# Splitting a scan chunk's rows 3 to 5 between VectorE and GpSimd, with C in two fixed PSUM banks

## The chip, the cores and the metric

The kernel runs on one core of a Trainium2 chip. The metric is the device time of one execution in microseconds (us), as a median of several runs. Engine names in the profile are PE (TensorE), DVE (VectorE), ACT (ScalarE), POOL (GpSimd) and SP (the engine that issues most DMAs).

## The reference, cut to what matters

Two layers work on eight images of 128 x 128 points with 128 channels, x[8, 128, 128, 128] in float32. The first is a linear attention with a layer norm. The second is a state-space layer with 256 inner channels and one state per channel. The change lies in the second layer's scan and the sum of its directions:

```python
xf = xb.reshape(Bb, Cd, L)
xt = jnp.transpose(xb, (0, 1, 3, 2)).reshape(Bb, Cd, L)
xs = jnp.stack([xf, xf[..., ::-1], xt, xt[..., ::-1]], axis=1)
...
dA = jnp.exp(dlt[..., None] * A[:, None])
xc = dA * xc + dut[..., None] * Bt[:, :, None, :]
y = jnp.einsum('kbcn,kbn->kbc', xc, Ct)
...
y = (y0 + y1 + y2 + y3).transpose(0, 2, 1)
yz = y * jax.nn.silu(z)
yn = gamma * (yz - mean(yz)) / sqrt(var(yz) + 1e-05) + beta
out = yn @ Wout
```

Every image is scanned along its rows and along its columns, forwards and backwards. Each scan's state is multiplied by C, which is one number for each point and the same for all channels, and the four results are added after they are turned back into one order of points. The last four lines are written shorter here than in the program.

## The kernel before, in words

There are three stages, one after the other: `layer0`, `layer1_front` and `layer1_scan`. The change is in `layer1_scan`, which the profile shows from about 4530 us to the end.

The 256 channels lie as 2 x 128 partitions. The sum `y` of one image, [128, 2, 16384], stays in SBUF. The work is a list of 8 x 4 slots, one for each image and each of its scans, and each slot is cut into 16 chunks of 1024 points, eight rows of 128. One chunk is one `step`; there are 512, and some 17 more in which the last image leaves. `place` (0 to 3) is the position of a slot in its image. The slot at place 0 writes `y`, and those at places 1, 2 and 3 add to it. In places 1 and 2 the points of the scan run along the other axis than the memory of `y` does; the program calls that `y_turned`. Then neighbours in the scan lie 128 elements (512 bytes) apart in `y`. At place 3 they don't.

In step n each engine does this, in an order written out by hand in `step`, which `in_order` keeps for each engine:

- PE makes the step sizes in PSUM (`delta`, L934) and spreads C over all partitions (`spread`, L967), one matmul for each half of a chunk.
- ACT makes softplus (`soften`, L938) and the decay (`decay`, L942) in place in PSUM, with a table load for each.
- POOL multiplies the input by the step sizes into `h` (`weigh`, L951), two instructions of 1024.
- DVE runs two scans over `h` (`scan`, L959 forwards, L961 with the other direction's views).

In the next step the chunk is given out. `emit` multiplies half of `h` (four rows, 2 x 512 elements) by C, on DVE. For the half that comes first the product goes to a PSUM buffer that the decays have left (L989 where y is turned, L993 where it isn't), and `gather` (L1001, DVE) adds it to `y`. The other half is multiplied in place (L982, DVE), and `add` (L1009, POOL) adds it to `y`, with one instruction of 512 elements for each half of the channels. So DVE adds four rows and POOL four. At place 0 both halves are written to `y` by DVE directly (L979).

The scan buffer `h` has two copies. The scan of chunk n starts from the last column of chunk n-1, so the copy of n-1 is free for n+1 only when both scans of n are done.

While the next image is at place 0, the image before leaves, one chunk in each step: `gate` (L1029) multiplies by z, `square` (L1032), `moments` (L1042) sums over the channels on PE, `keep` (L1048), `to_tokens` (L1054) turns the sums, `square_mean` (L1058) and `variance` (L1062) read them, `project` (L1074) is the output matmul, `store` (L1080) scales and stores. Such a step is called a leaving step.

[...] The pool `px` has three buffers of two banks each. The pool `pe` has two tags of one bank each. `spread` takes "pc" for the half that is emitted first and "pt" for the other, and the leaving image's `pm` and `pq` also take "pt":

```python
half1 = units[n][0].first
spread(n, half1, "pc")
spread(n, 1 - half1, "pt")
...
pm = pe.tile([P, GN], F32, name="pm", tag="pt")
pts[m] = p = pe.tile([P, GW, NC2, 2], F32, name="pq", tag="pt")
```

Of the kernel before, what the change touches and what calls it, by code (L numbers as in the profile page):

```python
# [8 lines left out]
F32 = mybir.dt.float32  # L9
BF16 = mybir.dt.bfloat16  # L10
AF = mybir.ActivationFunctionType
ALU = mybir.AluOpType
# [4 lines left out]
P = 128  # L17
B = 8
H = W = 128
L = H * W  # L20
NH, HD = 4, 32
NC2 = 2
R = 8
K = 4
GW = 4
GN = GW * H
# [5 lines left out]
CW = CH // H  # L32
NCH = L // CH
# [714 lines left out]
def layer1_scan(ctx: ExitStack, tc, ubs, xps, zs, gs, dtw, dtb, a_log, gamma, beta, w_out, out):  # L748
# [15 lines left out]
    nc = tc.nc  # L764
# [4 lines left out]
    px = ctx.enter_context(tc.tile_pool(name="l2px", bufs=3, space=PSUM))  # L769
    pe = ctx.enter_context(tc.tile_pool(name="l2pe", bufs=1, space=PSUM))  # L770
# [14 lines left out]
    for dst, src, rows in ((wparts, dtw.rearrange("k r d -> r k d"), R), (bparts, dtb.rearrange("o (k d) -> o k d", d=D2), 1)):  # L785
        x = wp.tile([rows, K, D2], F32, name="w32", tag="sp", bufs=2)
        nc.sync.dma_start(x, src)
        q = wp.tile([rows, 3, K, D2], BF16, name="w16", tag="h", bufs=2)
# [13 lines left out]
    rws, dws = [], []  # L802
    for i in range(3):
        t = const.tile([P, CH], BF16, name=f"rows{i}")
# [3 lines left out]
    for i in range(3):  # L808
        t = const.tile([P, D2], BF16, name=f"dtw{i}")
        nc.gpsimd.memset(t, 0.0)  # L810
        dws.append(t)
    csel = const.tile([P, P], BF16, name="csel")
# [17 lines left out]
    for j in range(2):  # L830
        for hf in range(2):
            at = 32 * (2 * j + hf)
            nc.vector.memset(sel[at : at + 1, hf, j : j + 1], 1.0)
    pb = pe.tile([P, P], F32, name="pbw", tag="pt")
    for c in range(NC2):
        bt = wp.tile([P, P], F32, name="bt", tag="z", bufs=6)
        nc.vector.tensor_copy(bt, gb[:, 1, c : c + 1].to_broadcast([P, P]))
# [2 lines left out]
    nc.vector.tensor_copy(bw, pb)  # L840
    for c in range(NC2):
        nc.vector.tensor_scalar(wg[:, c, :], wg[:, c, :], gb[:, 0, c : c + 1], None, ALU.mult)
    pb = pe.tile([P, P], F32, name="pbm", tag="pt")
    for c in range(NC2):
        nc.tensor.matmul(pb, means, wg[:, c, :], start=(c == 0), stop=(c == NC2 - 1))
    for c in range(NC2):
# [2 lines left out]
    y = big.tile([P, NC2, L], F32, name="y")  # L849
    yturn = y.rearrange("p c (w h) -> p c h w", h=H)  # L850

    class Slot:


        def __init__(self, n, o, s):
            self.o, self.s = o, s
            self.b, self.k = o // 4 + 2 * s, o % 4
            self.back = self.k % 2 == 1
            self.order = NAT if self.k >= 2 else TURN
            self.permuted = self.order != (TURN if self.b < B // 2 else NAT)  # L860
            self.dt_image, dt_dir = 2 * self.k + self.b // 4, self.b % 4
            self.dt_order = NAT if dt_dir >= 2 else TURN
            self.dt_turned_back = self.back != (dt_dir % 2 == 1)
            self.y_turned = (self.order == TURN) != (s < 2)
            self.y_back = s % 2 == 1
            self.place = n % K

            self.first = 1 if self.place and not self.back else 0
            self.dw = dws[n % 3]

        def weights(self):
# [8 lines left out]

            return NCH - 1 - i if self.back else i

        def y_at(self, i, hf):

            m = 2 * self.at(i) + hf
            if self.y_back:
                m = 2 * NCH - 1 - m
            if self.y_turned:
                v = yturn[:, :, m * GW : m * GW + GW, :]
            else:  # L890
                v = y[:, :, m * GN : m * GN + GN].rearrange("p c (a b) -> p c a b", b=H)
            return v[:, :, ::-1, ::-1] if self.y_back else v


# [1 line left out]
    units = []  # L896
    for o in range(B):
        for s in ([3, 0, 1, 2] if o % 4 >= 2 else [1, 2, 3, 0]):
            sl = Slot(len(units) // NCH, o, s)
            units += [(sl, i) for i in range(NCH)]  # L900

    ubt, sp, da, hs = {}, {}, {}, {}
# [57 lines left out]
        else:  # L960
            nc.vector.tensor_tensor_scan(e, x, e, start, ALU.mult, ALU.add)  # L961

    cps, ts = {}, {}

    def spread(n, hf, tag):
        cps[n, hf] = p = pe.tile([P, 1, GN], F32, name="pc", tag=tag)
        nc.tensor.matmul(p[:, 0, :], csel, rws[n % 3][:, hf * 512 : hf * 512 + 512], start=True, stop=True)  # L967

    def emit(n, hf):

        sl, i = units[n]
        h = hs[n][:, :, hf * 512 : hf * 512 + 512]
        c = cps.pop((n, hf)).to_broadcast([P, NC2, GN])
        if sl.place == 0:
            v = sl.y_at(i, hf)
            split = "p c (a b) -> p c a b"
            nc.vector.tensor_tensor(v, h.rearrange(split, b=H), c.rearrange(split, b=H), ALU.mult)  # L979
            return  # L980
        if hf != sl.first:
            nc.vector.tensor_tensor(h, h, c, ALU.mult)  # L982
            return
        p = da.pop((n, 1))
        if sl.y_turned:
            ts[n] = p.rearrange("p (c b a) -> p c b a", c=NC2, a=GW)
            t = p.rearrange("p (c b a) -> p c a b", c=NC2, a=GW)
            split = "p c (a b) -> p c a b"
            nc.vector.tensor_tensor(t, h.rearrange(split, b=H), c.rearrange(split, b=H), ALU.mult)  # L989
        else:  # L990
            t = p.rearrange("p (c q) -> p c q", c=NC2)
            ts[n] = t.rearrange("p c (a b) -> p c a b", b=H)
            nc.vector.tensor_tensor(t, h, c, ALU.mult)  # L993

    def gather(n):

        sl, i = units[n]
        v = sl.y_at(i, sl.first)
        if sl.y_turned:
            v = v.rearrange("p c a b -> p c b a")  # L1000
        nc.vector.tensor_tensor(v, v, ts.pop(n), ALU.add)  # L1001

    def add(n):
        sl, i = units[n]
        hf = 1 - sl.first
        h = hs[n][:, :, hf * 512 : hf * 512 + 512].rearrange("p c (a b) -> p c a b", b=H)
        v = sl.y_at(i, hf)
        for c in range(NC2):
            nc.gpsimd.tensor_tensor(v[:, c], v[:, c], h[:, c], ALU.add)  # L1009


    zt, rst, pts, mv = {}, {}, {}, {}
# [20 lines left out]

    def moments(m):

        pm = pe.tile([P, GN], F32, name="pm", tag="pt")
        for c in range(NC2):
            for j in range(2):
                for hf in range(2):
                    at = 32 * (2 * j + hf)  # L1040
                    v = piece(m, hf) if j else zt[m, hf]
                    nc.tensor.matmul(pm[at : at + 32, :], mean, v[:, c, :], start=(c == 0), stop=(c == NC2 - 1))  # L1042
        pts[m, "rows"] = pm
# [5 lines left out]

    def to_tokens(m):  # L1050
        sr = pts.pop((m, "rows"))
        pts[m] = p = pe.tile([P, GW, NC2, 2], F32, name="pq", tag="pt")
        for w in range(GW):
            nc.tensor.matmul(p[:, w], sr[:, w * H : w * H + H], sel, start=True, stop=True)  # L1054

# [35 lines left out]
    for o in range(B):  # L1091
        n = (o + 1) * K * NCH
# [14 lines left out]
    def step(n):  # L1107
        live = 0 <= n < N
        then = n + 1 < N
        before = 1 <= n <= N  # L1110
        now, last, soon, later = (leaving.get(n + i) for i in (0, -1, 1, 2))
        first = before and units[n - 1][0].place == 0
        if before:
            half1 = units[n - 1][0].first
            emit(n - 1, half1)
            if not first:
                gather(n - 1)
        if now and last:
            gate(*now, 1, nc.vector)
        if before:  # L1120
            emit(n - 1, 1 - half1)
        if n + 2 < N:
            load_rows(n + 2)
        if n in fetched:
            fetch(*fetched[n])
        if live:
            decay(n, 0)
        if now:
            square(now[1], 1)
        if live:  # L1130
            decay(n, 1)
            weigh(n, 0)
            if n + 2 < N:
                load(n + 2, 0)
        if last:
            deviation(last[1])
        if live:
            weigh(n, 1)
            if n + 2 < N:
                load(n + 2, 1)  # L1140
        if now:
            moments(now[1])
        if live:
            scan(n, 0)
            da.pop((n, 0))
        if last:
            for hf in range(2):
                store(*last, hf)
        if then:
            for c in range(NC2):  # L1150
                delta(n + 1, c)
        if now:
            keep(now[1])
        if then:
            soften(n + 1, 0)
        if now:
            to_tokens(now[1])
            square_mean(now[1])
        if then:
            soften(n + 1, 1)  # L1160
        if live:
            scan(n, 1)
        if first:
            hs.pop(n - 1)
        if now:
            variance(now[1])
        if live:
            half1 = units[n][0].first
            spread(n, half1, "pc")
            spread(n, 1 - half1, "pt")  # L1170
        if soon and now:
            gate(*soon, 0, nc.gpsimd)
        elif soon:
            gate(*soon, 1, nc.gpsimd)
        elif later:
            gate(*later, 0, nc.gpsimd)
        if soon:
            square(soon[1], 0)
        if now:
            p = da.pop((n, 1)) if live else px.tile([P, CH], F32, name="px")  # L1180
            for hf in range(2):
                project(now[1], hf, p[:, hf * 512 : hf * 512 + 512])
        elif live and units[n][0].place == 0:
            da.pop((n, 1))
        if before and not first:
            add(n - 1)
            hs.pop(n - 1)
        if n in weighed:
            units[weighed[n]][0].weights()
        if n in summed:  # L1190
            add_d(*summed[n])
# [78 lines left out]
```

## Time and profile before

| | us |
|---|---|
| median of 3 runs | 9257.28 (9252.85 to 9259.84) |
| the profiled execution | 9261.02 |
| its span in the trace | 9259.2 |
| DVE busy | 7992.0 (86%) |
| POOL busy | 7316.5 (79%) |
| ACT busy | 7099.7 (77%) |
| PE busy | 6337.5 (68%) |

A group line of the profile gives the source line, engine, operation, output and inputs, shapes and count, then the busy time and the mean of one in ns, and then the idle time of the engine before them with what ended it. A line of the timeline gives the start, the duration, the engine, the source line and the operation; the idle time before it stands in brackets. Shares of busy time are means over stages with different limits, so that a change in one stage has to be read from that stage.

### The profile page before, as it was taken

Reading aid. Unit: us, or ns where it says so; the run is one execution under the profiler, and the core shown is the slowest. Engines: PE = TensorE matmul, PEld = TensorE weight load, DVE = VectorE, ACT = ScalarE, POOL = GpSimd, SP = SyncE. Lnnn points to the kernel's source line nnn. Section 1 sums busy time; section 2 is a strip of 40 time slices with the busy share of each in tenths; the row PEclk is TensorE's granted clock in tenths of the full one; section 3 lists DMA queues with packets and bytes.
Section 4 is the critical chain, followed back from the end, with each engine's and each line's share of the span. In section 5 each row is a group of like instructions: output and inputs, shape, how many; then the busy total and the mean of one; then the engine's idle time right before and its main releaser. Section 6 shows DMA issues by size and latency. Waiting matters only on the chain. (4 is left out here: it accounts for less than half of the span.)

```text
span 9259.2 us, 91316 instructions
## 1 busy us (share of the span) xinstructions
PE 6337.5 (68%) x24512; PEld 3096.6 (33%) x24512; DVE 7992.0 (86%) x7953; ACT 7099.7 (77%) x8066; POOL 7316.5 (79%) x4684
## 2 busy tenths in 40 slices
PE   8899998988899999999434636446364463643636
PEld 5555555554333333333101304114031140311403
DVE  6667666774699999999799999999999999999996
ACT  5555555657789999999688887887878888888885
POOL 3446444554588988888599899998999989999897
PEclk9999999999999999999655757557575575755857
DMA  1322333123478789888758769587695876957767
GB/s 76 146 84 96 137 121 146 70 109 137 148 242 249 251 246 244 245 246 241 206 154 238 208 185 258 158 230 216 179 260 159 222 225 178 257 165 218 230 174 211
DMA packets 934769, 1750.66 MB, mean 189 GB/s; under 512 B 150228, under 2 KB 376148, under 8 KB 926064
## 3 DMA queue, kind: packets, MB, share of 16 engines
q1 hardware_dynamic: 873328, 1509.92, 49.4%
q0 software_dynamic: 60928, 234.90, 13.8%
q8 instruction: 200, 3.28, 0.1%
q14 instruction: 313, 2.56, 0.1%
HBM read 1052.36 MB, written 692.12 MB: 188 GB/s over the span
## 5 line engine op out<-in xcount | busy, mean ns | idle before, releaser
L951 POOL TENSOR_TENSOR h<-ubt,sp 128x1024 f32<-128x1024 f32 x1024 | 2422.4, 2399 | 348.4 <-ACT mv L1058 124.1
L934 PE MATMUL px<-rows,dtw 128*128 128x512 bf16 x2048 | 953.5, 565 | 2266.2 <-DVE y L1001 1084.5
L534 DVE SCALAR_TENSOR_TENSOR acc<-xb,cw,acc 128x1024 f32<-128x1024 f32 x1024 | 1320.3, 1289 | 133.7 <-ACT xb L502 89.9
L526 POOL TENSOR_TENSOR tap<-tap 128x1024 f32<-128x1024 f32 x512 | 1224.0, 2394 | 243.9 <-ACT tap L524 220.6
L938 ACT ACTIVATE sp<-px 128x1024 f32<-128x1024 f32 x1024 | 1047.3, 1024 | 435.4 <-PE px L934 418.1
L961 DVE TENSOR_TENSOR_SCAN h<-px,h 128x1024 f32<-128x1024 f32 x512 | 1177.3, 2331 | 31.7 <-ACT px L942 15.1
L934 PEld LDWEIGHTS <-dtw 128*128 128x128 bf16 x2048 | 169.1, 110 | 3089.1 <-issue 1022.7
L959 DVE TENSOR_TENSOR_SCAN h<-px,h 128x1024 f32<-128x1024 f32 x512 | 1177.9, 2330 | 21.4 <-POOL h L951 18.8
L1009 POOL TENSOR_TENSOR y<-y,h 128x512 f32<-128x512 f32 x768 | 1159.8, 1559 | 3.8 <-DVE h L982 3.8
L942 ACT ACTIVATE px<-sp,sa 128x1024 f32<-128x1024 f32 x1024 | 1110.4, 1109 | 6.1
L515 PE MATMUL acc<-xi,wt 128*128 128x512 f32 x2048 | 938.3, 601 | 53.7 <-ACT ures L539 53.7
L524 ACT ACTIVATE tap<-xb,cw 128x1024 f32<-128x1024 f32 x768 | 837.3, 1139 | 15.2 <-POOL xb L499 15.1
L282 POOL TENSOR_TENSOR q<-q,qs 128x512 f32<-128x512 f32 x256 | 272.2, 1063 | 695.5 <-DVE qs L281 695.5
L938 ACT ACT_TABLE_LOAD x512 | 656.9, 1283 | 170.0 <-PE px L934 168.0
L942 ACT ACT_TABLE_LOAD x512 | 656.9, 1283 | 9.1
L1074 PEld LDWEIGHTS px<-wg,z 128*128 128x128 f32 x4096 | 575.3, 225 | 114.8 <-issue 109.1
L1074 PE MATMUL px<-wg,z 128*128 128x128 f32 x4096 | 574.7, 308 | 0.0
L967 PE MATMUL pc<-rows,csel 128*128 128x512 bf16 x1024 | 517.5, 586 | 78.2 <-DVE rstd L1062 74.5
L515 PEld LDWEIGHTS acc<-xi,wt 128*128 128x128 f32 x2048 | 375.1, 189 | 574.4 <-issue 411.9
L488 PE MATMUL pxb<-xi,wi 128*128 128x512 f32 x1024 | 496.2, 607 | 2.1 <-ACT xb L497 2.1
L298 ACT ACTIVATE sq<-o 128x512 f32<-128x512 f32 x256 | 161.2, 630 | 421.0 <-DVE o L296 419.8
L1001 DVE TENSOR_TENSOR y<-y,px 128x1024 f32<-128x1024 f32 x384 | 468.6, 1220 | 14.4
(153 smaller groups left out, 15038.8 us busy)
## 6 DMA issues: line engine op xcount, KB each, us to landing
ubt<-ubs SPq DMA_DIRECT2D x1024, 512.0 KB
zs<-z SPq DMA_DIRECT2D x512, 256.0 KB
ubs<-ures SPq DMA_DIRECT2D x256, 512.0 KB
ubs<-turned SPq DMA_DIRECT2D x256, 512.0 KB
z<-zs SPq DMA_DIRECT2D x256, 512.0 KB
y<-gs POOLq DMA_DIRECT2D x128, 1024.0 KB, 10.3
gs<-du POOLq DMA_DIRECT2D x96, 1024.0 KB, 8.6
rows<-xps SPq DMA_DIRECT2D x1536, 60.0 KB
```

The lines of the kernel that those rows point to most:

```text
L515: nc.tensor.matmul(acc[:, s, :], wt[:, j, c, :], x, start=(j == 0), stop=(j == len(ON_PE) - 1))
L524: nc.scalar.activation(t, at(n, c, *d), AF.Copy, scale=weight(n, c, *d))
L526: nc.gpsimd.tensor_tensor(sums[n, c], sums[n, c], t, ALU.add)
L534: nc.vector.scalar_tensor_tensor(acc, at(n, c, *d), weight(n, c, *d), acc, ALU.mult, ALU.add)
L934: nc.tensor.matmul(p[:, hf * 512 : hf * 512 + 512], sl.dw[:, c * P : c * P + P], src, start=True, stop=True)
L938: nc.scalar.activation(t, da[n, c], AF.Softplus)
L942: nc.scalar.activation(da[n, c], sp[n, c], AF.Exp, scale=sa[:, sl.s, c : c + 1])
L951: nc.gpsimd.tensor_tensor(h, u, t, ALU.mult)
L959: nc.vector.tensor_tensor_scan(e[:, ::-1], x[:, ::-1], e[:, ::-1], start, ALU.mult, ALU.add)
L961: nc.vector.tensor_tensor_scan(e, x, e, start, ALU.mult, ALU.add)
L1009: nc.gpsimd.tensor_tensor(v[:, c], v[:, c], h[:, c], ALU.add)
L1074: nc.tensor.matmul(po[:, w, :], z[:, c, w * H : w * H + H], wg[:, c, :], start=(c == 0), stop=(c == NC2 - 1))
```

## The change

Where y is turned and the place is not 0, a chunk's eight rows are no longer cut in halves of four. The part that DVE multiplies into PSUM and gathers has three rows, and the part that POOL adds has five. POOL's add there is written with y's neighbours in memory innermost: 128 runs of five, where it was four runs of 128 with a step of 512 bytes. Then `h` is read with that step. Where y isn't turned, and at place 0, the parts stay at four rows.

As a part of five rows reaches over both halves of a chunk, C is no longer held in two tiles. One tile `cs` of two banks is made once, and `spread` writes half 0 to its first bank and half 1 to its second. `moments` and `to_tokens` use views of the second bank. Two tiles that are used once at the start come from the pool `px`.

```diff
@@ Slot.__init__
             self.first = 1 if self.place and not self.back else 0
+            r = (3 if self.y_turned else GW) if self.place else GW
+            self.rows = ((CW - r, CW), (0, CW - r)) if self.first else ((0, r), (r, CW))
@@ y_at
-        def y_at(self, i, hf):
-            m = 2 * self.at(i) + hf
+        def y_at(self, i, part):
+            r0, r1 = (CW * self.at(i) + r for r in self.rows[part])
...
-                v = yturn[:, :, m * GW : m * GW + GW, :]
+                v = yturn[:, :, r0:r1, :]
@@ spread, emit
-    def spread(n, hf, tag):
-        cps[n, hf] = p = pe.tile([P, 1, GN], F32, name="pc", tag=tag)
-        nc.tensor.matmul(p[:, 0, :], csel, rws[n % 3][:, hf * 512 : hf * 512 + 512], start=True, stop=True)
+    cs = pe.tile([P, 2, GN], F32, name="cs")
+    def spread(n, hf):
+        nc.tensor.matmul(cs[:, hf, :], csel, rws[n % 3][:, hf * 512 : hf * 512 + 512], start=True, stop=True)
+    def tokens(n, part):
+        r0, r1 = units[n][0].rows[part]
+        return slice(r0 * H, r1 * H)
...
-        h = hs[n][:, :, hf * 512 : hf * 512 + 512]
-        c = cps.pop((n, hf)).to_broadcast([P, NC2, GN])
+        s = tokens(n, part)
+        h = hs[n][:, :, s]
+        c = cs.rearrange("p (o f) q -> p o (f q)", o=1)[:, :, s].to_broadcast([P, NC2, s.stop - s.start])
...
-        p = da.pop((n, 1))
+        p = da.pop((n, 1)).rearrange("p (c q) -> p c q", c=NC2)[:, :, 0 : s.stop - s.start]
         if sl.y_turned:
-            ts[n] = p.rearrange("p (c b a) -> p c b a", c=NC2, a=GW)
-            t = p.rearrange("p (c b a) -> p c a b", c=NC2, a=GW)
+            ts[n] = p.rearrange("p c (b a) -> p c b a", b=H)
+            t = p.rearrange("p c (b a) -> p c a b", b=H)
@@ add
-        hf = 1 - sl.first
-        h = hs[n][:, :, hf * 512 : hf * 512 + 512].rearrange("p c (a b) -> p c a b", b=H)
-        v = sl.y_at(i, hf)
+        h = hs[n][:, :, tokens(n, 1)].rearrange("p c (a b) -> p c a b", b=H)
+        v = sl.y_at(i, 1)
+        if sl.y_turned:
+            v, h = (t.rearrange("p c a b -> p c b a") for t in (v, h))
         for c in range(NC2):
             nc.gpsimd.tensor_tensor(v[:, c], v[:, c], h[:, c], ALU.add)
@@ moments, to_tokens
-        pm = pe.tile([P, GN], F32, name="pm", tag="pt")
+        pm = cs[:, 1, :]
...
-        pts[m] = p = pe.tile([P, GW, NC2, 2], F32, name="pq", tag="pt")
+        pts[m] = p = cs[:, 1, 0 : GW * NC2 * 2].rearrange("p (w h t) -> p w h t", w=GW, h=NC2)
@@ step
-            half1 = units[n - 1][0].first
-            emit(n - 1, half1)
+            emit(n - 1, 0)
...
-            emit(n - 1, 1 - half1)
+            emit(n - 1, 1)
...
-            spread(n, half1, "pc")
-            spread(n, 1 - half1, "pt")
+            spread(n, half1)
+            spread(n, 1 - half1)
```

More of the change, by code (lines that the diff above doesn't have):

```diff
@@ L833, in layer1_scan @@
             nc.vector.memset(sel[at : at + 1, hf, j : j + 1], 1.0)
-    pb = pe.tile([P, P], F32, name="pbw", tag="pt")
+    pb = px.tile([P, P], F32, name="pbw", tag="px")
     for c in range(NC2):
@@ L842, in layer1_scan @@
         nc.vector.tensor_scalar(wg[:, c, :], wg[:, c, :], gb[:, 0, c : c + 1], None, ALU.mult)
-    pb = pe.tile([P, P], F32, name="pbm", tag="pt")
+    pb = px.tile([P, P], F32, name="pbm", tag="px")
     for c in range(NC2):
@@ L881, in at @@
             return NCH - 1 - i if self.back else i
-        def y_at(self, i, hf):
-            m = 2 * self.at(i) + hf
+        def y_at(self, i, part):
+            r0, r1 = (CW * self.at(i) + r for r in self.rows[part])
             if self.y_back:
-                m = 2 * NCH - 1 - m
+                r0, r1 = H - r1, H - r0
             if self.y_turned:
-                v = yturn[:, :, m * GW : m * GW + GW, :]
+                v = yturn[:, :, r0:r1, :]
             else:
-                v = y[:, :, m * GN : m * GN + GN].rearrange("p c (a b) -> p c a b", b=H)
+                v = y[:, :, r0 * H : r1 * H].rearrange("p c (a b) -> p c a b", b=H)
             return v[:, :, ::-1, ::-1] if self.y_back else v
@@ L961, in scan, with emit @@
             nc.vector.tensor_tensor_scan(e, x, e, start, ALU.mult, ALU.add)
-    cps, ts = {}, {}
-    def spread(n, hf, tag):
-        cps[n, hf] = p = pe.tile([P, 1, GN], F32, name="pc", tag=tag)
-        nc.tensor.matmul(p[:, 0, :], csel, rws[n % 3][:, hf * 512 : hf * 512 + 512], start=True, stop=True)
-    def emit(n, hf):
+    cs = pe.tile([P, 2, GN], F32, name="cs")
+    ts = {}
+    def spread(n, hf):
[3 more added lines that the diff above has]
+        return slice(r0 * H, r1 * H)
+    def emit(n, part):
         sl, i = units[n]
-        h = hs[n][:, :, hf * 512 : hf * 512 + 512]
-        c = cps.pop((n, hf)).to_broadcast([P, NC2, GN])
+        s = tokens(n, part)
+        h = hs[n][:, :, s]
+        c = cs.rearrange("p (o f) q -> p o (f q)", o=1)[:, :, s].to_broadcast([P, NC2, s.stop - s.start])
+        split = "p c (a b) -> p c a b"
         if sl.place == 0:
-            v = sl.y_at(i, hf)
-            split = "p c (a b) -> p c a b"
+            v = sl.y_at(i, part)
             nc.vector.tensor_tensor(v, h.rearrange(split, b=H), c.rearrange(split, b=H), ALU.mult)
             return
-        if hf != sl.first:
+        if part:
             nc.vector.tensor_tensor(h, h, c, ALU.mult)
             return
-        p = da.pop((n, 1))
+        p = da.pop((n, 1)).rearrange("p (c q) -> p c q", c=NC2)[:, :, 0 : s.stop - s.start]
         if sl.y_turned:
-            ts[n] = p.rearrange("p (c b a) -> p c b a", c=NC2, a=GW)
-            t = p.rearrange("p (c b a) -> p c a b", c=NC2, a=GW)
-            split = "p c (a b) -> p c a b"
+            ts[n] = p.rearrange("p c (b a) -> p c b a", b=H)
+            t = p.rearrange("p c (b a) -> p c a b", b=H)
             nc.vector.tensor_tensor(t, h.rearrange(split, b=H), c.rearrange(split, b=H), ALU.mult)
         else:
-            t = p.rearrange("p (c q) -> p c q", c=NC2)
-            ts[n] = t.rearrange("p c (a b) -> p c a b", b=H)
-            nc.vector.tensor_tensor(t, h, c, ALU.mult)
+            ts[n] = p.rearrange(split, b=H)
+            nc.vector.tensor_tensor(p, h, c, ALU.mult)
     def gather(n):
         sl, i = units[n]
-        v = sl.y_at(i, sl.first)
+        v = sl.y_at(i, 0)
         if sl.y_turned:
@@ L1004, in add @@
         sl, i = units[n]
-        hf = 1 - sl.first
-        h = hs[n][:, :, hf * 512 : hf * 512 + 512].rearrange("p c (a b) -> p c a b", b=H)
-        v = sl.y_at(i, hf)
+        h = hs[n][:, :, tokens(n, 1)].rearrange("p c (a b) -> p c a b", b=H)
+        v = sl.y_at(i, 1)
+        if sl.y_turned:
+            v, h = (t.rearrange("p c a b -> p c b a") for t in (v, h))
         for c in range(NC2):
```

## The prediction

> **What bounds the kernel now.** I read the page first for the shares, then the windows to cut the scan stage into its kinds of step, then the timeline of one step of each kind the change touches. In the page VectorE (DVE) is busiest, but only on average:
>
> ```profile
> PE 6337.5 (68%) x24512; PEld 3096.6 (33%) x24512; DVE 7992.0 (86%) x7953; ACT 7099.7 (77%) x8066; POOL 7316.5 (79%) x4684
> L1009 POOL TENSOR_TENSOR y<-y,h 128x512 f32<-128x512 f32 x768 | 1159.8, 1559 | 3.8 <-DVE h L982 3.8
> ```
>
> The change touches the scans alone (from about 4530 us to the end). There the windows show two regimes:
>
> ```profile
> core 0: us, PE busy (x) PEld busy (x) DVE busy (x) ACT busy (x) POOL busy (x), PEclk, DMA share, GB/s
> 5932.00:6030.00 98.00, 34.78 (x72) 8.23 (x72) 96.27 (x61) 80.66 (x72) 93.55 (x48) 0.50 0.52 150
> 8614.26:8625.54 11.28, 8.19 (x62) 6.05 (x62) 11.23 (x14) 9.60 (x11) 9.87 (x5) 1.00 1.04 296
> ```
>
> The first is a stretch of steps in which y is turned; the second is one step in which the previous image leaves. VectorE is full in both. In the turned stretch GpSimd (POOL) has only 6% left, and that decides this case. The timeline there, one step of 8.22 us:
>
> ```profile
> 6009.02 1.23 DVE L989 TENSOR_TENSOR px<-h,pc 128x1024 f32<-128x1024 f32 x1
> 6009.15 4.66 POOL L951 TENSOR_TENSOR h<-ubt,sp 128x1024 f32<-128x1024 f32 x2 [0.38 <-DVE h L961]
> ...
> 6010.29 1.22 DVE L1001 TENSOR_TENSOR y<-y,px 128x1024 f32<-128x1024 f32 x1
> 6011.43 1.21 DVE L982 TENSOR_TENSOR h<-h,pc 128x1024 f32<-128x1024 f32 x1
> ...
> 6012.56 4.58 DVE L961 TENSOR_TENSOR_SCAN h<-px,h 128x1024 f32<-128x1024 f32 x2
> 6013.77 3.23 POOL L1009 TENSOR_TENSOR y<-y,h 128x512 f32<-128x512 f32 x2
> ...
> 6017.24 1.23 DVE L989 TENSOR_TENSOR px<-h,pc 128x1024 f32<-128x1024 f32 x1
> ```
>
> VectorE runs emit, gather, emit, scan, scan without a gap. GpSimd works 7.85 us (6009.15 to 6017.00) and then waits 0.38 us for the last scan, because the next `h` takes the buffer whose last column that scan reads. So a turned step lasts max(VectorE 8.22, GpSimd about 7.8 when it never waits).
>
> The leaving step, around its variance:
>
> ```profile
> 8613.24 0.38 PE L967 MATMUL pc<-rows,csel 128*128 128x512 bf16 x1
> ...
> 8614.12 0.14 DVE L1062 TENSOR_TENSOR rstd<-pq,mv 128x8 f32<-128x8 f32 x1
> 8614.31 1.22 DVE L979 TENSOR_TENSOR y<-h,pc 128x1024 f32<-128x1024 f32 x1
> 8614.31 0.38 PE L967 MATMUL pc<-rows,csel 128*128 128x512 bf16 x1 [0.70 <-DVE rstd L1062]
> ```
>
> The reader is to see that the first C matmul ran a microsecond ahead in its own bank, so VectorE went from the variance to the emit in 0.05 us. Only the second matmul waited for the variance, whose bank it reuses, and it hid behind the emit.
>
> [...] packed adds of 512 took 1.272 us (median of L1009 where y isn't turned, 4940 to 5030 us), products of 1024 took 2.359 us (median of L951), so 2.12 ns an element[...] and 0.185 us fixed. [...] the strided copies of L606 took 1.091 us for 512 and 2.004 us for 1024, 1.78 ns an element, while the packed casts of L44 took 0.398 us for 256, some 0.85 ns if the same 0.18 us is fixed. [...] All of VectorE's operations in a turned step have their other input in PSUM, and their times are steady[...].
>
> **The change, part by part.** Of each image's four scans, two are turned: 8 x 2 x 16 = 256 steps.
>
> *VectorE in a turned step.* L989 and the gather L1001 go from 1024 to 768 elements, L982 from 1024 to 1280. [...] they become 0.96, 0.95 and 1.48 us: 3.39 instead of 3.66, so 0.27 less, and the step would be 7.95 us. Against it: the gather now touches y in runs of three[...]. Bounds: nothing, to 0.3 us, at which the saving is gone. I take nothing, because it matters only if VectorE still sets the pace.
>
> *GpSimd in a turned step.* Two adds go from 512 to 640 elements, and walk y in runs of five and `h` with a step of 512 bytes; before, y was read and written with that step and `h` was packed. Before: 1.641 us (median in the turned stretches), so (1.641 - 0.185)/512 = 2.84 ns an element, 0.72 above packed. What will 640 take? Lower bound: hopping on a read costs nothing and all 0.72 was the write: 0.185 + 640 x 2.12 = 1.54 us. Same rate: 0.185 + 640 x 2.84 = 2.00 us. Upper bound: broken runs of y cost on top, 2.15 us, an estimate. [...] L606 beside L44 shows that reads pay; that speaks for 2.00. [...] I take **1.95 us**. A GpSimd step that never waits is then 4.62 + 2 x 1.95 - 0.09 (overlaps seen between neighbours: 2 x 1.641 shows as 3.23, and weigh follows add with about 0.04) = 8.43 us. That exceeds 8.22, so GpSimd becomes the bound: 0.21 x 256 = **+54 us**. The point where it turns is 1.85 us an add (8.22); from 1.71 us downwards VectorE sets 7.95. Bounds: -69 us (1.71 or less) to +156 us (2.15). Nothing else moves in these steps: scans wait for GpSimd instead, PE and ScalarE have 20% and more to spare.
>
> *C in two fixed banks.* C, `pm` and `pq` are now views of one tile, `cs`. In the built program of the changed kernel the first of the two C matmuls in a leaving step waits for the variance, although it writes the other bank, and the emit waits for the second. So the matmul that ran ahead no longer does. VectorE, with everything after the emit queued behind it (gate, second emit, scan), stands still for both: a pair of such matmuls takes 0.59 us at full clock and 1.01 at half (pairs of L934 at 8612.00 and at 6011.56), plus some 0.04 of hand-over, against 0.05 now. At full clock that is about 0.63 us, at half about 1.05; the granted clock in leaving stretches is 0.84 to 0.93, so about 0.75. There are 7 x 16 = 112 such steps (the eighth image leaves with no scan beside it): 84 us. In some two dozen of them VectorE waits anyway, for `out` stores (L1080, 42 us in 19 waits, some in the tail) or for GpSimd; the delay vanishes there, about 16 us. Net **+68 us**, bounds 50 to 90. PE's projection starts as much later, but its result is wanted a scan later: nothing.
>
> *In other steps* both C matmuls end about 0.3 us before the last scan does, so waiting for both costs nothing; if that cover were gone it would cost 0.3 us. `pbw` and `pbm` move to other banks, once at the start: nothing. No DMA is added or moved; the loads on SP's queue follow the same releases.
>
> **Sum.** 54 + 68 = +122 us on the profiled execution's own 9261.0, so 9383. The median of the runs is 9257.3, 3.7 lower: 9380 us.
>
> **Rivals.** (1) *GpSimd's add is cheap*: at 1.71 us or less VectorE sets 7.95 us, -69 us, and the stall gives back 68: about 9257, not slower. This one ends on the other side; its mechanism is the write hop, its place the 256 turned steps, its deciding point 1.71 us. For it: the strided write is gone; against: L606's copies pay for a strided read with a packed write. If the stall is at its low end too, it is 9240. (2) *The whole rate moves with h*: 2.00 us to 2.15, +79 to +156, with the stall 9405 to 9481. (3) *The leaving steps hide the stall* (DMA share there is near 1, and stores are waited for): +54 alone, 9311. Against: VectorE's 11.23 of 11.28 us. (4) *The runs of three eat VectorE's saving* with a cheap add: turned steps unchanged, +68, 9325.
>
> **Numbers.** Likeliest case, add at 1.86 to 2.00 with the stall: 0.4 (9330 to 9410). Rival 2: 0.24. Rivals 3 and 4, and adds between 1.71 and 1.86: 0.11. Rival 1: 0.25, of which 0.17 falls within 0.2% and 0.08 below it. Range 9250 to 9455: it leaves out rival 1 with a small stall, and an add above some 2.09 us, together under 0.2. About 0.2% (18 us) is what a measurement can tell from no change: faster 0.08, same 0.17, slower 0.75.
>
> **What would show it.** In the changed profile: the add on GpSimd near 1.95 us; its idle time before L951 in turned steps gone, GpSimd near 99% and VectorE near 93% in those windows, steps of 8.4 us; in leaving steps a gap of 0.6 to 1 us on VectorE before the emit, put down to PE, and steps near 11.9 us. Wrong if turned steps are 8.0 us (the add below 1.71), or if the emit still follows the variance at once.

## The result and the profile after

The changed kernel takes **9352.69 us** (median of 4 runs, 9351.37 to 9352.91) against 9257.34 before: ratio 1.0102, 95% interval 1.009 to 1.0115, so 95 us slower. The forecast was 9380, slower. The direction and the size hold, but the two terms of its sum do not: the turned steps cost more than forecast and the leaving steps far less. In what follows the changed kernel's lines are numbered a little later: L951 became L953, L961 L963, L967 L969, L979 L986, L982 L989, L989 L995, L1001 L1006, L1009 L1015, L1029 L1035, L1058 L1064, L1062 L1068.

The first two rows are from the page of the changed kernel, shares by engine and the add's group (busy time, mean ns, idle before):

```profile
PE 6347.9 (68%) x24512; PEld 3085.0 (33%) x24512; DVE 7891.6 (84%) x7953; ACT 7094.5 (76%) x8066; POOL 7470.0 (80%) x4684
L1015 POOL TENSOR_TENSOR y<-y,h 128x640 f32<-128x640 f32 (+1 forms) x768 | 1340.6, 1812 | 2.0 <-DVE h L989 1.9
```

VectorE lost 100 us of work and GpSimd gained 154, yet the shares hardly moved. The windows show where it counts. This is a turned stretch of the changed kernel (columns as in the prediction):

```profile
6520.00:6618.00 98.00, 32.91 (x68) 6.41 (x68) 90.89 (x59) 78.18 (x70) 97.06 (x47) 0.50 0.50 143
```

The busy times are us in a stretch of 98 us. So GpSimd is busy for 99% (97.06 of 98), up from 95.5% (93.55), and VectorE is down from 98% (96.27) to 93% (90.89): the bound has changed hands. The timeline of a turned step in the changed kernel, GpSimd's rows first:

```profile
6053.07 4.66 POOL L953 TENSOR_TENSOR h<-ubt,sp 128x1024 f32<-128x1024 f32 x2
6057.68 3.88 POOL L1015 TENSOR_TENSOR y<-y,h 128x640 f32<-128x640 f32 x2
6061.64 4.66 POOL L953 TENSOR_TENSOR h<-ubt,sp 128x1024 f32<-128x1024 f32 x2
```

```profile
6060.22 0.96 DVE L995 TENSOR_TENSOR px<-h,cs 128x768 f32<-128x768 f32 x1
6061.22 0.95 DVE L1006 TENSOR_TENSOR y<-y,px 128x768 f32<-128x768 f32 x1
6062.09 1.48 DVE L989 TENSOR_TENSOR h<-h,cs 128x1280 f32<-128x1280 f32 x1
6064.03 4.66 DVE L963 TENSOR_TENSOR_SCAN h<-px,h 128x1024 f32<-128x1024 f32 x2 [0.46 <-POOL h L953]
```

A step lasts 8.57 us (6053.07 to 6061.64), and now the scan waits for GpSimd's product, 0.46 us, where GpSimd used to wait 0.38 us for the scan. VectorE's three operations are as short as forecast (0.96, 0.95 and 1.48).

The leaving step, first VectorE and then GpSimd, in the changed kernel:

```profile
8752.94 0.14 DVE L1068 TENSOR_TENSOR rstd<-cs,mv 128x8 f32<-128x8 f32 x1
8753.76 1.22 DVE L986 TENSOR_TENSOR y<-h,cs 128x1024 f32<-128x1024 f32 x1 [0.68 <-PE cs L969]
8754.89 1.71 DVE L1035 TENSOR_TENSOR z<-y,z 128x1024 f32<-128x1024 f32 x1
8756.53 1.21 DVE L986 TENSOR_TENSOR y<-h,cs 128x1024 f32<-128x1024 f32 x1
...
8764.23 0.14 DVE L1068 TENSOR_TENSOR rstd<-cs,mv 128x8 f32<-128x8 f32 x1
```

```profile
8753.15 2.37 POOL L953 TENSOR_TENSOR h<-ubt,sp 128x1024 f32<-128x1024 f32 x1 [1.34 <-ACT mv L1064]
```

and the gate and the product at the same place before the change (the emit ahead of them, L979 at 8614.31, is shown in the prediction):

```profile
8615.44 2.34 DVE L1029 TENSOR_TENSOR z<-y,z 128x1024 f32<-128x1024 f32 x1
```

```profile
8614.35 2.36 POOL L951 TENSOR_TENSOR h<-ubt,sp 128x1024 f32<-128x1024 f32 x1 [0.43 <-ACT mv L1058]
```

The stall is there, 0.68 us put down to PE. But from variance to variance the step is 11.29 us, as it was (11.28). What gave it back is the gate: 2.34 us before, 1.71 after. In both kernels it ends 1.07 to 1.08 us after GpSimd's product does (8617.78 against 8616.71; 8756.60 against 8755.52). The same holds for every gate among VectorE's first 112 that took over 1.3 us, 105 of them before and 69 after: each ends 1.08 to 1.09 us after an instruction of GpSimd. This suggests that the gate was never 2.34 us of work: it waited for GpSimd, and a gate that starts 0.63 us later ends at the same moment. The experiments put that to the test.

By slots (from the start of one slot's first scan to the next slot's, summed over eight images) places 1 and 2 grew from 2120.1 to 2194.2 us (74), place 3 by 5.7 and place 0, where images leave, by 16.9; start and tail give back 5. That makes the 92 us by which the span grew.

### The profile page after: what moved, and what is told of

Its sections match the earlier page's. It is cut to its first block, busy times and chain, and to the rows that moved or that the text cites. A ratio compares the mean times of both kernels' runs of the same rounds, so it can differ in the third digit from the quotient of the medians.

```text
span 9350.8 us, 91626 instructions
## 1 busy us (share of the span) xinstructions
PE 6347.9 (68%) x24512; PEld 3085.0 (33%) x24512; DVE 7891.6 (84%) x7953; ACT 7094.5 (76%) x8066; POOL 7470.0 (80%) x4684
## 3 DMA queue, kind: packets, MB, share of 16 engines
q8 instruction: 201, 3.29, 0.1%
## 5 line engine op out<-in xcount | busy, mean ns | idle before, releaser
L953 POOL TENSOR_TENSOR h<-ubt,sp 128x1024 f32<-128x1024 f32 x1024 | 2427.8, 2420 | 289.9 <-ACT mv L1064 130.0
L1015 POOL TENSOR_TENSOR y<-y,h 128x640 f32<-128x640 f32 (+1 forms) x768 | 1340.6, 1812 | 2.0 <-DVE h L989 1.9
L963 DVE TENSOR_TENSOR_SCAN h<-px,h 128x1024 f32<-128x1024 f32 x512 | 1187.1, 2341 | 79.0 <-POOL h L953 63.1
L961 DVE TENSOR_TENSOR_SCAN h<-px,h 128x1024 f32<-128x1024 f32 x512 | 1188.0, 2341 | 66.5 <-POOL h L953 65.5
L936 PEld LDWEIGHTS <-dtw 128*128 128x128 bf16 x2048 | 141.9, 106 | 3181.3 <-issue 884.9
L1080 PEld LDWEIGHTS px<-wg,z 128*128 128x128 f32 x4096 | 584.4, 227 | 25.7 <-issue 10.7
L969 PE MATMUL cs<-rows,csel 128*128 128x512 bf16 x1024 | 505.8, 594 | 109.3 <-DVE rstd L1068 105.3
L989 DVE TENSOR_TENSOR h<-h,cs 128x1280 f32<-128x1280 f32 (+1 forms) x384 | 534.6, 1392 | 0.0
```

The source lines that it names most:

```text
L936: nc.tensor.matmul(p[:, hf * 512 : hf * 512 + 512], sl.dw[:, c * P : c * P + P], src, start=True, stop=True)
L953: nc.gpsimd.tensor_tensor(h, u, t, ALU.mult)
L961: nc.vector.tensor_tensor_scan(e[:, ::-1], x[:, ::-1], e[:, ::-1], start, ALU.mult, ALU.add)
L1080: nc.tensor.matmul(po[:, w, :], z[:, c, w * H : w * H + H], wg[:, c, :], start=(c == 0), stop=(c == NC2 - 1))
```

## The experiments

My theory (A): the turned steps are bound by GpSimd, at 2 x 1.96 us for the adds plus a wait that the forecast left out, and the stall in the leaving steps is hidden behind the gate's own wait. All ratios stand against runs of the kernel before on the same chip. Differences from the changed kernel cross two sets of runs, in which the kernel before took 9257.34 and 9255.02 us, so they are good to some 2 us. In kernels without the new walk the lines from the add on stand two earlier, so that the gate is L1033.

**C in two fixed banks, and nothing else.**

```diff
-            r = (3 if self.y_turned else GW) if self.place else GW
+            r = GW
...
-        if sl.y_turned:
-            v, h = (t.rearrange("p c a b -> p c b a") for t in (v, h))
```

> The changed kernel with four and four rows and the old walk: of the change only C's two fixed banks are left. Theory A (the stall in the leaving steps is hidden: VectorE's gate, L1035 there, has to wait for GpSimd's product anyway, so a later start ends at the same time): the emit starts 0.63 to 1.1 us after the variance as in the changed kernel, the gate gets shorter by as much, leaving steps stay at 11.28 us, the time is within 15 us of the kernel before (about 9260). Theory B (the stall was paid and something else in the changed kernel gave it back): leaving steps near 11.9 us, about 68 us slower than before.

Measured: 9263.23 us, ratio 1.001 (1.0003 to 1.0016), turned steps 8.22 us and leaving steps 11.29. The emit starts 0.85 us after the variance in the mean of the 112 steps (0.04 before), and VectorE's gate goes from a mean of 2.25 to 1.61 us (over the first 112 of its 120). A step with a wait of 1.10 us, as the changed kernel has where the pair of C matmuls takes 1.01 us at a granted clock of 0.50 (at 8764.42) and not 0.59 at 1.00 (at 8753.13, in the step shown above); VectorE and then GpSimd:

```profile
8680.39 1.22 DVE L986 TENSOR_TENSOR y<-h,cs 128x1024 f32<-128x1024 f32 x1 [1.10 <-PE cs L969]
8681.53 1.28 DVE L1033 TENSOR_TENSOR z<-y,z 128x1024 f32<-128x1024 f32 x1
```

```profile
8679.37 2.36 POOL L953 TENSOR_TENSOR h<-ubt,sp 128x1024 f32<-128x1024 f32 x1 [1.34 <-ACT mv L1062]
```

Even after a stall of 1.10 us the gate ends 1.08 us after GpSimd's product (8682.81 against 8681.73). The fixed banks cost some 8 us (3 to 15 by the interval), not 68. Theory B falls.

**Five rows on the old walk.**

```diff
-        if sl.y_turned:
-            v, h = (t.rearrange("p c a b -> p c b a") for t in (v, h))
```

> The changed kernel with GpSimd's five rows walked as before (y with a step of 512 bytes, h packed). Theory A (the cost of hopping lies on the reads, so it only moved from y to h): 2.0 us an add against 1.96, the turned step 0.1 us longer than the changed kernel's 8.55, the time about 25 us above it (9378). Rival (the new walk is what made five rows bearable, the old one costs far more for five): an add of 2.2 us or more, over 120 us above the changed kernel.

Measured: 9365.49 us (1.0108 to 1.0136), 13 us above the changed kernel where 25 were expected, with turned steps of 8.63 us. The add takes 2.00 us (shown below) against 1.96, so the rival, 2.2 us or more, falls.

**The new walk on four rows.**

```diff
-            r = (3 if self.y_turned else GW) if self.place else GW
+            r = GW
```

> The changed kernel with four and four rows everywhere, the new walk (runs of four in y). Theory A (same rate as with five rows, (1.956-0.185)/640 = 2.77 ns an element): 1.60 us an add against 1.64 before; VectorE sets the turned step, 8.22 us, the time is that of the kernel with fixed banks alone. Rival (runs of five pay for their odd word, runs of four do not): an add near 1.5 us, the same time.

Measured: 9265.36 us (1.0005 to 1.0018), as with the banks alone. The add's own durations in a turned stretch (minimum, median and maximum in ns), for the changed kernel, five rows on the old walk, and four on the new:

```profile
L1015 POOL TENSOR_TENSOR y<-y,h x16: 1950/1964/1978, 6032.0 to 6093.9; 128x640 f32<-128x640 f32 x16
```

```profile
L1013 POOL TENSOR_TENSOR y<-y,h x17: 1962/1997/2025, 6028.9 to 6098.0; 128x640 f32<-128x640 f32 x17
```

```profile
L1015 POOL TENSOR_TENSOR y<-y,h x18: 1249/1514/1549, 6030.5 to 6097.4; 128x512 f32<-128x512 f32 x18
```

The walk by itself does help, and more with runs of four: at four rows 1.51 us against 1.64, at five only 1.96 against 2.00. With the same fixed 0.185 us these are 2.60 and 2.78 ns an element on the new walk, against 2.84 on the old one. The rival's guess for four rows (near 1.5) was the better one: runs of five cost more an element than runs of four (2.78 ns against 2.60). Why was not shown: no run here separates a run's length from where in y it starts. No walk with a hop that was seen here brings five rows under 1.71 us: at 2.60 ns they would take 1.85. Only the packed rate, 2.12, would (1.54).

**One of the two adds left away.**

```diff
-        for c in range(NC2):
+        for c in range(1 if sl.y_turned else NC2):
             nc.gpsimd.tensor_tensor(v[:, c], v[:, c], h[:, c], ALU.add)
```

> The changed kernel, with GpSimd's second add (the second half of the channels) left out where y is turned; those parts of the sum are missing in the output. Theory A (GpSimd sets the turned step): the step falls from 8.55 to VectorE's 7.95 us, 0.6 x 256 = 154 us below the changed kernel, about 9200 and so some 57 us below the kernel before. Rival (VectorE or PE sets it too, for instance by the runs of three in the gather): the step stays above 8.2 us.

Measured: 9205.62 us, ratio 0.9947 (0.9935 to 0.9959), 147 us below the changed kernel; part of the sum is missing from this kernel's output, so it serves as a measurement only. VectorE in a turned step:

```profile
6034.25 0.96 DVE L995 TENSOR_TENSOR px<-h,cs 128x768 f32<-128x768 f32 x1
6035.24 0.95 DVE L1006 TENSOR_TENSOR y<-y,px 128x768 f32<-128x768 f32 x1
6036.12 1.48 DVE L989 TENSOR_TENSOR h<-h,cs 128x1280 f32<-128x1280 f32 x1
6037.51 4.58 DVE L963 TENSOR_TENSOR_SCAN h<-px,h 128x1024 f32<-128x1024 f32 x2
6042.20 0.96 DVE L995 TENSOR_TENSOR px<-h,cs 128x768 f32<-128x768 f32 x1
```

The step is 7.95 us (6034.25 to 6042.20), with no gap. So the saving on VectorE is real, and GpSimd alone keeps it from showing. The gather's runs of three cost nothing: 0.95 us for 768 elements, as forecast.

**The gate behind the second emit, in the kernel before.**

```diff
-        if now and last:
-            gate(*now, 1, nc.vector)
         if before:
             emit(n - 1, 1 - half1)
+        if now and last:
+            gate(*now, 1, nc.vector)
```

> The kernel before, with VectorE's gate moved behind the second emit in a leaving step. Theory A (the gate's 2.34 us are 1.2 us of waiting for GpSimd's product and 1.1 us of work): the gate then starts after that product has ended and takes about 1.1 to 1.2 us; VectorE's step falls from 11.28 to about 10.2 us, but ScalarE's decay is ready only some 0.6 us earlier than the scan starts now, so the step is about 10.7 us where DMA allows it; about 40 to 60 us faster than the kernel before. Rival (2.34 us is what this product of two SBUF tensors takes on VectorE): the gate stays at 2.3 us and the time does not move.

Measured: **9214.27 us**, ratio 0.9954 (0.9941 to 0.9968), which beats both kernels. VectorE, and GpSimd's product:

```profile
8634.64 2.35 DVE L979 TENSOR_TENSOR y<-h,pc 128x1024 f32<-128x1024 f32 x2
8636.91 1.22 DVE L1029 TENSOR_TENSOR z<-y,z 128x1024 f32<-128x1024 f32 x1
8638.32 2.35 DVE L959 TENSOR_TENSOR_SCAN h<-px,h 128x1024 f32<-128x1024 f32 x1 [0.20 <-POOL rstd L1066]
```

```profile
8634.67 2.37 POOL L951 TENSOR_TENSOR h<-ubt,sp 128x1024 f32<-128x1024 f32 x1 [0.49 <-issue]
```

Here the gate starts as GpSimd's product ends (8636.91 against 8637.04). It takes 1.22 us, and less than 1.4 us in 83 of the 112 steps. So the long gates were waits, as theory A has it. The median leaving step falls to 10.46 us, a little further than the 10.7 I expected.

**The same move, with C in two fixed banks.** (The edit is that of the last one, on the kernel of the first experiment.)

> C in two fixed banks, four and four rows, old walk, and the gate behind the second emit. Theory A (the fixed banks' stall of 0.63 to 1.05 us is only hidden by the gate's wait): with that wait gone the stall shows, the leaving step is 0.5 to 0.6 us longer than in the kernel that moves the gate alone, some 40 to 60 us in all, and close to the kernel before (9250). Rival (the stall is hidden by something else, DMA or ScalarE): within 15 us of the kernel that moves the gate alone.

Measured: 9243.98 us (0.9976 to 0.9992), 30 us above the kernel that moves the gate alone, a little less than expected; the median leaving step is 10.80 against 10.46 us. With its cover gone, the stall shows:

```profile
8627.12 2.35 DVE L986 TENSOR_TENSOR y<-h,cs 128x1024 f32<-128x1024 f32 x2 [0.68 <-PE cs L969]
8629.39 1.22 DVE L1033 TENSOR_TENSOR z<-y,z 128x1024 f32<-128x1024 f32 x1
8630.53 2.34 DVE L961 TENSOR_TENSOR_SCAN h<-px,h 128x1024 f32<-128x1024 f32 x1
```

This shows that the gate's wait covered the stall: take that wait away, and the fixed banks cost 30 us where they had cost 8. But it isn't the forecast's 68. The emit starts 0.78 us later in the mean of the 112 steps (0.82 against 0.03 us after the variance), and the median step grows by only 0.34. Part of the stall still falls into other waits: in the kernel that moves the gate alone the scan stands still for 0.20 us anyway (above), and here for none. What takes the rest was not measured.

**The gate ahead of the first emit**, in the kernel before and with fixed banks:

```diff
+        if now and last:
+            gate(*now, 1, nc.vector)
         if before:
...
-        if now and last:
-            gate(*now, 1, nc.vector)
         if before:
```

> The kernel before, with VectorE's gate moved ahead of the first emit, right behind the variance. Theory A (whoever starts first runs, the other waits): the gate starts some 0.05 us after the variance, about as early as GpSimd's product, which is released a little later; the gate takes 1.1 us and the product is delayed by as much (3.4 us in the trace), still early enough for the scan; step about 10.7 us, 40 to 60 us faster than the kernel before. If GpSimd starts first, the gate takes 2.3 to 3.4 us and nothing is won.

> C in two fixed banks, four and four rows, old walk, and the gate ahead of the first emit. Theory A: the gate covers the wait for both C matmuls, so the fixed banks cost nothing: within 15 us of the kernel that moves the gate to the same place without them. Rival: the stall adds 40 us or more.

Measured: 9225.95 us (0.9953 to 0.9978) and 9246.83 us (0.998 to 0.9993). Both have a median leaving step of 10.44 us, and with fixed banks the emit follows the gate without a gap in all 105 steps that have one between the variance and the emit: there the gate does cover the wait for C. Now GpSimd waits for VectorE. In the usual step, here of the kernel without fixed banks, the gate starts first, and GpSimd's product takes 3.29 instead of 2.36 us:

```profile
8628.32 1.21 DVE L1029 TENSOR_TENSOR z<-y,z 128x1024 f32<-128x1024 f32 x1
8628.48 3.29 POOL L951 TENSOR_TENSOR h<-ubt,sp 128x1024 f32<-128x1024 f32 x1 [0.87 <-ACT mv L1058]
```

But the two differ by 21 us, more than I expected. In some steps GpSimd starts first and the gate takes about 3 us (23 of the 112 steps without fixed banks, 26 with them). One with fixed banks:

```profile
8626.50 2.36 POOL L953 TENSOR_TENSOR h<-ubt,sp 128x1024 f32<-128x1024 f32 x1 [0.78 <-ACT mv L1062]
8626.61 3.33 DVE L1033 TENSOR_TENSOR z<-y,z 128x1024 f32<-128x1024 f32 x1
```

The mean of VectorE's first 112 gates is 1.77 us with fixed banks and 1.66 without. Whether the banks make that more frequent or the runs merely fell so is left open.

**Three buffers for h, in the changed kernel.**

```diff
-            hs[n] = wp.tile([P, NC2, CH], F32, name="h", bufs=2)
+            hs[n] = wp.tile([P, NC2, CH], F32, name="h", bufs=3)
...
-            zt[m, hf] = z = wp.tile([P, NC2, GN], F32, name="z", bufs=6)
+            zt[m, hf] = z = wp.tile([P, NC2, GN], F32, name="z", bufs=4)
...
-            fetched[n + j - (2 if j > 2 else NCH + 4)] = e
+            fetched[n + j - (2 if j > 1 else NCH + 4)] = e
```

> The changed kernel with three buffers for h instead of two, so that GpSimd's product waits neither for its own last add nor for the scans. For the room z has four buffers instead of six, and one chunk of z is fetched later, so the leaving steps may get slower; the turned steps are what is read. Theory A (the 0.12 us by which the changed kernel's turned step of 8.57 us exceeds the 8.45 of the forecast is the product's wait for the add before it, as h's buffer is taken over): the product starts some 0.04 us before the add ends, as the add does after the product, and the turned step is 8.44 us. Rival (a GpSimd instruction with another access pattern costs 0.1 us to start, whatever it waits for): the step stays at 8.57 us.

Measured: 10196.8 us, since the leaving steps, with fewer buffers for z, take 20.4 us. The turned steps are the point, on GpSimd:

```profile
6202.46 4.70 POOL L953 TENSOR_TENSOR h<-ubt,sp 128x1024 f32<-128x1024 f32 x2
6207.08 3.92 POOL L1015 TENSOR_TENSOR y<-y,h 128x640 f32<-128x640 f32 x2
6210.91 4.70 POOL L953 TENSOR_TENSOR h<-ubt,sp 128x1024 f32<-128x1024 f32 x2
```

The step is 8.45 us here and 8.44 in the median. The product now starts 0.09 us before the add ends (6210.91 against 6211.00), where in the changed kernel it starts 0.08 us after it (6061.64 against 6061.56).

## Why the prediction was right, and where it was not

*The bound changes hands: right.* It named GpSimd as the engine that would set the turned step, an add of 1.95 us (measured 1.96), and 1.85 us as the point from which GpSimd sets a longer step than before. It also named GpSimd near 99% busy and VectorE near 93%, as measured. The scan's new wait for the product and the step of 7.95 us with half of the adds show both sides.

*The turned step's length: mechanism right, one term mis-sized.* The forecast said 8.43 us, measured 8.57. The term is the overlap between neighbours: I took 0.04 us of overlap for the step from the add to the next product as well. The trace before shows that overlap only from a product to the add behind it (6013.81 against 6013.77); after the add, the product stood still for the scan. That product takes over the buffer of `h` which the add just read, and must see the add complete; it starts 0.08 us after the add's end. (Some 0.02 us of the difference is the two adds, 1.96 for 1.95.) With a third buffer a step of 8.44 us appears. Times 256 steps, the missed 0.14 us is 36 us on paper, and 54 would have become 90; places 1 and 2 grew by 74. The difference lies in the slots at place 1: their second and third steps still take VectorE's 7.95 us and the fourth 8.45, probably because GpSimd has no adds at place 0 and enters place 1 ahead. With place 3, whose first step gives out a turned chunk, the slots grew by 80.

*VectorE's side: right.* 0.96, 0.95 and 1.48 us; taking nothing for the runs of three was right. The reason given for it was only that VectorE would not set the pace; that they cost nothing is what the runs add. No run shown ahead of the forecast gives the rate behind its three figures; the changed kernel does, 1.04 ns an element: L989 took 1.215 us for 1024 and 1.481 for 1280, and the gather, 1.221 for 1024 without runs of three and 0.954 for 768 in runs of three, lies on the same slope.

*The cost of the walk: right in the result, by chance.* My 1.95 us was an estimate a little below the 2.00 of an unchanged rate, and no run then showed how the hop's cost is shared between read and write. The runs show that on the new walk the rate depends on the run, 2.60 ns for four and 2.78 for five, both above packed (2.12) and below the old walk (2.84). One reading is that most of the hop's cost follows the read that hops, a part goes away with the hopping write, and runs of five give most of that part back. The split between read and write was not measured by itself, and the fixed 0.185 us is taken from the packed adds. The direction that L606 beside L44 gave, that stepped reads pay, fits, although those two differ in operation as well: all three walks read with a hop and exceed packed by 0.48 to 0.72 ns.

*The stall: there, nearly as priced, and wrong in its effect.* The emit starts 0.81 us later in the mean, where 0.75 was forecast. "VectorE, with everything after the emit queued behind it (gate, second emit, scan), stands still for both" is what happens (0.68 and 1.10 us). The step that failed is the next one, which added it to the path, 84 less 16 us. I read VectorE's 11.23 busy of 11.28 us as work, and set rival 3, that the leaving steps hide the stall, aside on that number; its reason (DMA) was also not the one. 1.1 us of that busy time was the gate waiting inside its own duration. So the fixed banks by themselves cost 8 us, and 30 where that wait was gone.

The traces show which of VectorE's operations waited like this. The gate reads two tensors in SBUF, y and z: 1.22 us alone, 2.34 beside the product. In the kernel before, four kinds with one operand in PSUM kept their time: the emit beside the same product took 1.22 us (L979 at 8614.31), all 256 of L979 1.205 to 1.223, and L989, L1001 and L982 1.228 to 1.230, 1.220 to 1.223 and 1.211 to 1.216 us. The prediction looked at the turned steps only, where all of VectorE's operations have one operand in PSUM.

The two errors had opposite signs. The stall was some 50 to 60 us too many: place 0 grew by 17 us in the profiled execution of the changed kernel, and by 5 to 18 in the five kernels that have fixed banks and the gate in its old place. The turned steps were some 26 us too few. So 9380 came near 9353 partly by luck.

One slip of reading in the prediction did no harm: GpSimd's 93.55 us of 98 leave 4.5% idle, not 6.

## What to carry to other kernels

Before moving work from the full engine to its neighbour, price the neighbour's instruction with its new access pattern and add it to the neighbour's own loop, waits for its own last instruction included: 4.5% of idle time does not take a quarter more of an add. An engine that shows 100% busy can still be waiting inside an instruction (1.1 of VectorE's 11.23 busy us in the leaving step): compare the same form's duration in other places, and where it is twice as long (2.34 us against 1.22), look at what the other engine is running at that moment. A wait that hides a new stall is also a gain not yet taken: moving the gate by one instruction brought 42 us, and made the fixed banks cost 30 us. And as two halves of one tile, C's two banks were ordered as one: in the leaving steps both matmuls waited for the variance (PE stood still for it 112 times, 105.3 us in all), where one of them had run ahead with two tiles.

## What the runs showed of the hardware

- A product of two SBUF tensors on VectorE (1024 elements) took 1.22 us alone and 2.34 us when GpSimd was 1.1 us into a 2.36 us instruction; whenever it took over 1.3 us it ended 1.08 to 1.09 us after an instruction of GpSimd (105 of 112 before the change), and the profile books the wait as busy time. The wait goes both ways: where VectorE's gate started first, GpSimd's product took 3.29 instead of 2.36 us.
- GpSimd's adds, with 0.185 us fixed taken for all: 2.12 ns an element packed, 2.84 with y read and written at a step of 512 bytes, 2.60 and 2.78 with `h` read at that step and y in runs of four and five.
- GpSimd's add began 0.04 us before the product ahead of it ended, and with three buffers for `h` the product 0.09 us before the add ended; where the product takes over the buffer that the add ahead of it reads, it began 0.08 us after that add's end.
- VectorE gathered y in runs of three without loss: 0.954 us for 768 elements, against 1.220 us for 1024 in runs of four, is the 1.04 ns an element that its product in place shows from 1024 to 1280 (1.215 and 1.481 us).
